# Moving the last two rows' key and value groups, and the output's bias parts, inside an integer attention

## The chip, the core and the metric

The kernel is one launch on one core of a Trainium2 chip. The metric is the device time of that launch in microseconds (us): the median of several runs. Beside it there is one profiled execution, from which every duration below comes. The engines are named as in the profile: PE is TensorE (matmuls and transposes), PEld its loading of weights, DVE is VectorE, ACT is ScalarE, POOL is GpSimd, and SP is SyncE, which issues nearly all DMAs. Each engine runs its own instructions in the order in which they were built, and waits for others by semaphores.

## The reference, cut to what matters

The program is a decoder of two layers, each an attention, a cross attention to media and a feed-forward part, on 8 rows of 512 positions with 256 channels. The change lies in the second layer's attention, which is computed in 8-bit integers, and touches the media attention behind it:

```python
x = x + _L1_attn_ref(_layernorm(x), ...)          # integer attention
x = x + _L1_xattn_ref(_layernorm(x), ctx_1024, ...)   # media attention
x = x + _L1_ffn_ref(_layernorm(x), ...)

# _L1_attn_ref, 16 heads of 16 channels
aw, aws = quant_act(einsum('ntd,nsd->nts', q, k), 8)
probs, ps = int_softmax(aw, aws, 8)
probs, ps = quant_act(probs, 8)
attn, as_ = quant_act(einsum('nts,nsd->ntd', probs, v), 8)   # one scale for all of attn
out = (einsum('tbi,oi->tbo', attn / as_, w_int) + round(b / b_s)) * b_s

# _L1_xattn_ref
k, v = split(media @ Wkv, 2, axis=-1)             # does not depend on x
```

`quant_act` takes the greatest absolute value of the whole tensor as its scale and rounds to integers. So the values of the attention (`attn`) can only be rounded when all of them are there. The keys and values of the media attention depend on `ctx_1024` and weights alone, and can be computed at any time before it.

## The kernel before, in words

**The integer attention** is `stage_quantized_attention`. Its last part runs through these stages, with the times of the profiled execution in us from the start of the span:

- scores (about 2170 to 2205), in eight blocks of 128 x 1024, kept in `aw`;
- softmax in integers (`integer_softmax`, 2205 to 2281), nearly all on DVE with exponents on ACT, ending in a global maximum, `ptop`, and its inverse `pr`;
- probability times value (2281 to 2333): a loop over nine iterations n. `spread(n)` copies the values of block n onto the diagonal of a zeroed tile `vz` (L2614, half on POOL, half on DVE). `turn(n)` rounds the probabilities (L2621, DVE), writes them four times, masked, into `qa_wide` (L2624, four ACT instructions), transposes them (L2632, 16 on PE) and copies the two PSUM tiles into `qa_pT` (L2635, DVE). `weigh(n - 1)` multiplies with the values (L2645, 64 small matmuls), copies the result to `m_` (L2653, ACT) and takes its maximum (L2654, DVE);
- the global maximum of the result and its scales (L2670 to L2678), then the **bias parts**: `bias_parts` (L2374 to L2383, ten DVE operations) rounds the output's bias and splits it into three bf16 parts in one row `brow`, which a matmul adds later; `orow` (L2686) is the row of output scales;
- rounding (about 2336 to 2352): eight blocks, each with one ACT instruction that adds a large constant (L2692), one DVE instruction that takes it off and writes bf16 (`qa_mi`, L2693), and eight transposes (L2696). After each second block eight small copies bring the transposed tiles from PSUM to `mT`; they go through `evac`, which takes ACT (L101) and DVE (L103) in turn;
- output (2351 to 2378): for each row eight matmuls (L2709) with four that add the bias (L2712), a scaling on DVE (`qa_o`, L2714), and the sum into `x` (L2716, on DVE or POOL).

**The media keys and values** of all 8 rows are computed ahead, inside that stage, by `keys_values`, a generator. One of its **groups** is one of four parts of a row's keys or of its values: two matmuls of 128 x 512 in f32 (L2756; each gives two records in the trace), a copy from PSUM to `kv_o`, a tile with three buffers (L2761, ACT), and a store of 256 KB to DRAM (L2762, SP). A row has eight groups, and takes one load of its context (L2733, SP). Row 0 is done during the scores. Rows 1 to 5 are done in the softmax: 40 groups, whose contexts lie in `room`, a large tile that is free then. Rows 6 and 7 are done in the value loop: two groups at the end of each of the first eight iterations, with one buffer, `kv_ctx`, for the context of both rows.

**What sets the order.** The code is recorded in program order, and a tile scheduler orders each engine's instructions; tiles come from pools, and a tile that takes the memory of an earlier one waits for the last use of that one (a store's landing included). Within an engine, the built order is what runs. In the built order of before, L2374 waits only for operations of DVE.

**The media attention**, `stage_media_attention`, starts with loads on SP (L2828, L2830, L2843 for keys and values of a row from DRAM, and L3022 for the router), and with normalizing `x` (L157).

Of the kernel before, what the change touches and what calls it, by code (L numbers as in the profile page):

```python
# [27 lines left out]
F32 = mybir.dt.float32  # L28
# [6 lines left out]
ALU = mybir.AluOpType  # L35
# [4 lines left out]
P = 128  # L40
B, S, C = 8, 512, 256
NST = S // P
# [1235 lines left out]
class FastDecoder(Decoder):  # L1278
# [1108 lines left out]
    def stage_quantized_attention(self, w):  # L2387
        nc, q = self.nc, self.q
        wT, ident, ones, magic = q["wT"], q["ident"], q["ones"], q["magic"]
        tc = self.tc  # L2390
        with tc.tile_pool(reuse_waits="tile", name="qa", bufs=1) as pool:
# [16 lines left out]
            brow = self.alloc(pool, [P, 3 * C], BF16, "qa_brow")  # L2408
            with tc.tile_pool(reuse_waits="tile", name="qa1", bufs=2) as tmp, tc.tile_pool(
                reuse_waits="tile", name="qp1", bufs=1, space=PSUM  # L2410
# [140 lines left out]
            with tc.tile_pool(reuse_waits="tile", name="qa2", bufs=1) as tmp, tc.tile_pool(  # L2551
                reuse_waits="tile", name="qp2", bufs=2, space=PSUM
# [6 lines left out]
                for n in range(8):  # L2559
# [6 lines left out]
                    for m in range(4):  # L2566
                        at = 4 * n + m
# [19 lines left out]
            with tc.tile_pool(reuse_waits="tile", name="qa3", bufs=2) as tmp, tc.tile_pool(  # L2587
                reuse_waits="tile", name="qp3", bufs=4, space=PSUM
            ) as psum:
                ptop = self.integer_softmax(tmp, aw, qs, atop)  # L2590
                room = self.alloc(pool, [P, 8, 2, S], F32, "qa_big")
                for _ in self.keys_values(tmp, psum, range(1, 6), room, "kv", 4):
                    pass

                ps_, _ = self.scaled(pool, ptop, 1.0 / 128.0 / 127.0, "qa_ps")
                pr = one("qa_pr")
                nc.vector.reciprocal(pr, ptop)
                nc.vector.tensor_scalar(pr, pr, 127.0, None, ALU.mult)


            m_ = self.alloc(pool, [P, 8, 4, C], F32, "qa_big")
            mtops = one("qa_mtops", 8)

            vz = h16("vz").rearrange("p (j i m a r d) -> p j i m a r d", j=2, i=NST, m=4, a=4, r=4)
# [1 line left out]
            with tc.tile_pool(reuse_waits="tile", name="qa4", bufs=2) as tmp, tc.tile_pool(  # L2606
                reuse_waits="tile", name="qp4", bufs=1, space=PSUM
            ) as psum:
                held = {}

                def spread(n):
                    for r in range(4):
                        rows_ = slice(32 * r, 32 * r + 32)
                        (nc.gpsimd if r < 2 else nc.vector).tensor_copy(  # L2614
                            vz[rows_, n % 2, :, :, :, r, :].rearrange("p i m a d -> p (i m) a d"),
                            vq[rows_, :, :, n].rearrange("p i m (a d) -> p (i m) a d", d=16),
                        )

                def turn(n):
                    a = aw[:, n]  # L2620
                    nc.vector.tensor_scalar(a, a, pr, MAGIC, ALU.mult, ALU.add)  # L2621
                    wide = self.alloc(tmp, [P, 16, 4, 4, B], BF16, "qa_wide")
                    for k in range(4):
                        nc.scalar.activation(  # L2624
                            wide[:, :, :, k, :].rearrange("p a r s -> p r a s"), a, AF.Identity,
                            bias=q["at_off"][:, k : k + 1], scale=q["at"][:, k : k + 1],
                        )
                    pT = held[n] = self.alloc(tmp, [P, 16, P], BF16, "qa_pT")
                    for half in range(2):
                        ps = self.alloc(psum, [P, 8, P], BF16, "tr", bufs=4)  # L2630
                        for i in range(8):
                            nc.tensor.transpose(  # L2632
                                ps[:, i], wide[:, 8 * half + i].rearrange("p r k s -> p (r k s)"), ident
                            )
                        nc.vector.tensor_copy(pT[:, 8 * half : 8 * half + 8], ps)  # L2635

                def weigh(n):
                    pT = held.pop(n)
                    po = self.alloc(psum, [P, 4, C], F32, "po", bufs=2)
                    for m in range(4):  # L2640
                        for a in range(4):
                            g, e = divmod(a, 2)
                            for st in range(NST):
                                rows_ = slice(32 * st, 32 * st + 32)
                                nc.tensor.matmul(  # L2645
                                    po[rows_, m, g * P : (g + 1) * P].rearrange("p (r e d) -> p e r d", e=2, d=16)[
                                        :, e
                                    ],
                                    pT[:, 4 * m + a, rows_],
                                    vz[:, n % 2, st, m, a].rearrange("p r d -> p (r d)"),  # L2650
                                    start=True, stop=True, skip_group_check=True,
                                )
                    nc.scalar.copy(m_[:, n], po)  # L2653
                    nc.vector.tensor_reduce(  # L2654
                        mtops[:, n : n + 1], m_[:, n], AX.XY, ALU.max, apply_absolute_value=True
                    )

                ahead = self.keys_values(tmp, psum, range(6, B), None, "tr", 4)
                for n in range(9):
                    if n < 8:  # L2660
                        spread(n)
                        turn(n)
                    if n:
                        weigh(n - 1)
                    for _ in range(2):
                        next(ahead, None)


            mtop = one("qa_mpart")
            nc.vector.tensor_reduce(mtop, mtops, AX.X, ALU.max)  # L2670
# [7 lines left out]
            nc.vector.reciprocal(osc_inv, osc)  # L2678
            mT = h16("mT").rearrange("p (c i t m) -> p c i t m", c=2, i=NST, t=B)
            brow = self.alloc(pool, [P, C], BF16, "qa_orow")  # L2680
            self.bias_parts(brow, q["rb"][:, 3 * C :], osc_inv, "qa_b")
            with tc.tile_pool(reuse_waits="tile", name="qa5", bufs=2) as tmp, tc.tile_pool(
                reuse_waits="tile", name="qp5", bufs=1, space=PSUM
            ) as psum:
                orow = self.alloc(tmp, [P, C], F32, "qa_orow_s", bufs=1)
                nc.vector.tensor_scalar(orow, q["wsc"][:, C:], osc, None, ALU.mult)  # L2686
                for n in range(0, 8, 2):
                    ps = [self.alloc(psum, [P, 8, P], BF16, "tr", bufs=4) for c in range(2)]
                    for h in range(2):
                        f = m_[:, n + h]  # L2690
                        mi = self.alloc(tmp, [P, 4, C], BF16, "qa_mi")
                        nc.scalar.activation(f, f, AF.Identity, bias=magic[:, 0:1], scale=mr)  # L2692
                        nc.vector.tensor_scalar(mi, f, -MAGIC, None, ALU.add)  # L2693
                        for c in range(2):
                            for m in range(4):
                                nc.tensor.transpose(  # L2696
                                    ps[c][:, 4 * h + m], mi[:, m, c * P : (c + 1) * P], ident
                                )
                    for c in range(2):
                        for st in range(NST):  # L2700
                            self.evac(
                                mT[:, c, st, :, 16 * n : 16 * n + 32].rearrange("p t (m k) -> p t m k", k=4),
                                ps[c][:, :, 32 * st : 32 * st + 32].rearrange("p m (k t) -> p t m k", t=B),
                            )
                for b in range(B):
                    ps = self.alloc(psum, [P, NST, C], F32, "pj", bufs=2)
                    for st in range(NST):
                        for c in range(2):
                            nc.tensor.matmul(  # L2709
                                ps[:, st], mT[:, c, st, b], wT[:, c, 3 * C :], start=(c == 0), stop=False  # L2710
                            )
                        nc.tensor.matmul(ps[:, st], ones[:, :P], brow, start=False, stop=True)  # L2712
                    o = self.alloc(tmp, [P, NST, C], F32, "qa_o")
                    nc.vector.tensor_tensor(o, ps, orow.unsqueeze(1).broadcast_to([P, NST, C]), ALU.mult)  # L2714
                    x = self.x[:, b * NST : (b + 1) * NST, :]
                    (nc.gpsimd if b in (2, 4, 6) else nc.vector).tensor_tensor(x, x, o, ALU.add)  # L2716
                    if b == 0:
                        self.media_stats = {b: self.twice_normal(tmp, b, self.const)}
        self.integers.close()

    def load_media_attention(self):
        self.w_media = super().load_media_attention()
        return self.w_media

    def keys_values(self, pool, psum, rows, room, tag, bufs, outs=None):

# [792 lines left out]
```

## Time and profile before

| What | us |
|---|---|
| median of 3 runs (3087.45, 3094.61, 3096.63) | 3094.61 |
| the profiled execution's own time | 3094.66 |
| its span, first to last instruction | 3092.7 |
| PE busy | 2842.4 (92%) |
| DVE busy | 2158.3 (70%) |
| ACT busy | 1155.1 (37%) |
| mean granted clock of PE | 0.974 |

The profiled execution is 2.0 us longer than its span. The profile page gives busy times over the whole program; the part that is changed takes some 170 us of it, so the views that matter are those of a stretch of time: busy times by stage, the chain of waits (the work that ended last, followed back to what released it), and the timeline. In a timeline line the first number is the start, the second the busy time, then engine, line and operation, output<-inputs, and in brackets the idle time before it and what ended it. `x8` is the number of instructions joined in a line.

### The profile page before, as it was taken

How to read it: one execution, taken by the hardware profiler on the slowest of the kernel's cores; microseconds unless marked ns; L12 is line 12 of the kernel's file. 1: busy time of each engine (PE TensorE's matmuls, PEld its weight loads, DVE VectorE, ACT ScalarE, POOL GpSimd, SP SyncE). 2: the span in 40 equal slices, each digit the busy share in tenths (PEclk: the TensorE clock that was granted, in tenths of full speed). 3: DMA queues.
4: the chain of work that ended last, by engine and by line, in shares of the span. 5: the costliest groups of instructions: out<-in, count | busy, mean ns of one | idle time of the engine just before them, and what ended most of it. 6: DMA issues, size and time to landing. Idle time of an engine off the chain costs nothing. (4 is left out here: it accounts for less than half of the span.)

```text
span 3092.7 us, 40203 instructions
## 1 busy us (share of the span) xinstructions
PE 2842.4 (92%) x14929; PEld 1507.6 (49%) x14944; DVE 2158.3 (70%) x4962; ACT 1155.1 (37%) x1623; POOL 409.6 (13%) x389
## 2 busy tenths in 40 slices
PE   8999999969999999999999999999786999997998
PEld 5653333225555556555555556555344334434665
DVE  7458999977887894357887898548788766665110
ACT  2237777724334321124344331115263443441111
POOL 1111111100001010000101111112111123231111
PEclk9999999989999999999999999999997999998999
DMA  7011212101001001001000012010332122223231
GB/s 242 1 35 50 71 49 70 36 19 56 15 15 29 15 24 36 0 1 43 22 15 22 22 38 69 14 41 28 125 122 76 52 93 83 90 69 96 98 139 61
DMA packets 130696, 168.74 MB, mean 55 GB/s; under 512 B 51760, under 2 KB 79665, under 8 KB 128442
## 3 DMA queue, kind: packets, MB, share of 16 engines
q1 hardware_dynamic: 126394, 154.48, 16.0%
q0 software_dynamic: 4096, 11.59, 1.0%
q8 instruction: 119, 1.95, 0.3%
q14 instruction: 87, 0.71, 0.1%
HBM read 113.12 MB, written 47.50 MB: 52 GB/s over the span
## 5 line engine op out<-in xcount | busy, mean ns | idle before, releaser
L1885 PE MATMUL pj<-w,la_hT 128*128 128x512 f32 x720 | 342.8, 615 | 32.7 <-DVE x L2062 16.3
L1732 DVE TENSOR_TENSOR x_e<-x_e,x_share 128x1024 f32<-128x1024 f32 x256 | 317.6, 1283 | 16.7 <-ACT x_e L1731 16.5
L1731 ACT ACTIVATE x_e<-sc 128x1024 f32<-128x1024 f32 x256 | 249.4, 1023 | 82.0 <-PE sc L1720 82.0
L1885 PEld LDWEIGHTS pj<-w,la_hT 128*128 128x128 f32 x720 | 131.7, 194 | 189.3 <-issue 118.1
L2007 ACT ACTIVATE la_e<-la_e 128x1024 f32<-128x1024 f32 (+1 forms) x128 | 121.1, 952 | 209.2 <-DVE la_e L2003 209.2
L2890 ACT ACTIVATE ma_e<-sc,ma_bias 128x1024 f32<-128x1024 f32 x128 | 135.8, 1110 | 165.3 <-PE sc L2884 165.3
L2216 ACT ACTIVATE lf_gate<-pj,lf_b 128x512 f32<-128x512 f32 (+1 forms) x82 | 56.3, 687 | 346.6 <-PE pj L2195 337.2
L2897 DVE TENSOR_TENSOR ma_esum<-ma_esum,ma_e 128x1024 f32<-128x1024 f32 x96 | 129.8, 1353 | 71.3 <-ACT ma_e L2890 34.8
L2195 PE MATMUL pj<-lf_hnT,w 128*128 128x512 f32 (+1 forms) x368 | 171.7, 595 | 0.6 <-DVE lf_hid L2221 0.6
L2003 DVE TENSOR_TENSOR la_e<-sc,la_mask 128x1024 f32<-128x1024 f32 (+1 forms) x128 | 137.0, 1081 | 41.1 <-PE sc L1995 41.0
L3262 POOL TENSOR_TENSOR la_oT<-la_o,x_wide 128x512 f32<-128x512 f32 x64 | 88.3, 1387 | 571.0 <-DMA x_wide<-invs 315.4
L1748 PE MATMUL po<-x_e,x_v 128*32 128x512 f32 x1024 | 138.1, 612 | 21.9 <-DVE x_e L1732 15.2
L2195 PE MATMUL sc<-lf_hnT,w 128*128 128x512 f32 x336 | 157.9, 592 | 0.0
L1720 PE MATMUL sc<-x_q,x_k 32*128 32x512 f32 x1024 | 151.3, 640 | 1.7 <-DVE sa_ok L1448 1.4
L2267 PE MATMUL po<-w,lf_hid 128*128 128x256 f32 x640 | 148.8, 379 | 0.0
L2221 DVE SCALAR_TENSOR_TENSOR lf_hid<-sc,lf_b,lf_gate 128x512 f32<-128x512 f32 x70 | 52.4, 748 | 126.9 <-PE sc L2195 126.9
L1995 PE MATMUL sc<-la_qkT 64*128 64x256 f32 (+1 forms) x1024 | 124.2, 373 | 12.3 <-ACT la_qkT L1931 11.3
L1892 ACT ACTIVATE la_sq<-pj 128x512 f32<-128x512 f32 x120 | 71.4, 595 | 170.3 <-PE pj L1885 170.3
L2057 PE MATMUL pj<-w,la_oT 128*128 128x256 f32 x512 | 122.3, 385 | 11.3 <-DVE x L2062 9.4
L2884 PE MATMUL sc<-ma_qT,ma_kT 64*128 64x512 f32 x512 | 129.9, 626 | 0.0
L2267 PEld LDWEIGHTS po<-w,lf_hid 128*128 128x128 f32 x640 | 117.8, 190 | 20.2 <-issue 6.7
L2908 PE MATMUL po<-ma_e,ma_v 128*64 128x512 f32 x512 | 124.2, 606 | 0.0
(493 smaller groups left out, 5296.2 us busy)
## 6 DMA issues: line engine op xcount, KB each, us to landing
x_wide<-invs SPq DMA_DIRECT2D x184, 128.0 KB
w<-in_f_w_dram SPq DMA_DIRECT2D x16, 1024.0 KB
kv<-kv_o SPq DMA_DIRECT2D x56, 256.0 KB
slots<-x_empty SPq DMA_DIRECT2D x8, 1028.0 KB
x_mask<-in_x_maskT_dram SPq DMA_DIRECT2D x8, 1024.0 KB
ma_kT<-kv SPq DMA_DIRECT2D x8, 1024.0 KB
ma_v<-kv SPq DMA_DIRECT2D x8, 1024.0 KB
ex_rows<-slots SPq DMA_DIRECT2D x7, 1028.0 KB
```

What stands on the lines that cost most here:

```text
L1720: nc.tensor.matmul(pair[r // 2][:, r % 2, :], d["k"][rows, g, kt * P : (kt + 1) * P], d["q"][rows, e, g, :], start=True, stop=True,)
L1731: nc.scalar.activation(ex, d["e"][rest][p], AF.Exp)
L1732: nc.vector.tensor_tensor(ex, ex, d["share"][:, kt, :].unsqueeze(1).broadcast_to([P, 2, 512]), ALU.mult)
L1748: nc.tensor.matmul(d["po"][32 * r : 32 * r + 32, :], d["v"][:, kt, 8 * g + 2 * r + e, :], ex[r // 2][:, r % 2, :], start=(kt == 0), stop=( ...
L1885: nc.tensor.matmul(ps, d["hT"][:, k, i * P : (i + 1) * P], wqkv[:, k, j * S : (j + 1) * S], start=(k == 0), stop=(k == 1),)
L1995: nc.tensor.matmul(both[half][:, r, jj * 256 : jj * 256 + to - j * P], d["qkT"][rows, 4 + c, j * P : (j + 1) * P], d["qkT"][rows, c, j * P ...
L2003: nc.vector.tensor_tensor(ex[:, :, :n_cols], ps[:, :, :n_cols], mask[:, :n_cols].unsqueeze(1).broadcast_to([P, 2, n_cols]), ALU.add,)
L2195: nc.tensor.matmul(ps[:m, :], w1[:, k, at : at + m], held[b]["hnT"][:, k, :], start=(k == 0), stop=(k == 1))
L2267: nc.tensor.matmul(ps[:, :C], held[b]["hid"][:, f, i * P : (i + 1) * P], w2[:, f, :], start=(f == 0), stop=False,)
L2884: nc.tensor.matmul(both[m // 2][:, r, :], d["k"][rows, c, kt * P : (kt + 1) * P], d["q"][rows, c, :], start=True, stop=True,)
L2890: nc.scalar.activation(ex, ps, AF.Exp, bias=bias[:, b * NST + kt : b * NST + kt + 1], scale=0.125)
L2897: nc.vector.tensor_tensor(d["sum", c], d["sum", c], ex, ALU.add)
```

## The change

Three things are changed in `stage_quantized_attention`:

- The sixteen groups of rows 6 and 7 are no longer made by the generator, but one at a time by a new function, `project`, from a list. Five are recorded at the end of the softmax, behind the 40 of rows 1 to 5. In the value loop one is recorded in each iteration but those with n = 3 and n = 7 (seven), and two behind the loop. The last two are recorded in the first two rows of the output. Row 6's context goes into `room`, row 7's into a tile of its own.
- The bias parts and the row of output scales are recorded behind the evacuations of the second pair of rounded blocks (n == 2), instead of ahead of all rounding.
- `m_`, which holds the result of the value loop, is a view of `room` instead of a new tile of the same tag.

In the built order of after, the five copies of the groups in the softmax stand ahead of the first L2624 on ACT; the bias parts are spread over DVE's order between the second L2693 and the seventh, among evacuations; and the tile that L2374 writes takes memory that `kv_o` of the value loop had.

```diff
@@ softmax
+                ctx6 = self.context(room[:, 5], 6)
+                groups = [(ctx6, 6, j, g) for j in range(2) for g in range(NST)]
+
+                def project(tmp, psum, tag, count=1):
+                    for group in groups[:count]:
+                        self.keys_values_group(tmp, psum, *group, tag, 4)
+                    del groups[:count]
+
+                project(tmp, psum, "kv", 5)
@@ ahead of the value loop
-            m_ = self.alloc(pool, [P, 8, 4, C], F32, "qa_big")
+            m_ = room.rearrange("p n a s -> p n (a s)").rearrange("p n (m c) -> p n m c", c=C)
+            stay = ExitStack()
+            late = stay.enter_context(tc.tile_pool(reuse_waits="tile", name="qx", bufs=1))
+            ctx7 = self.context(self.alloc(late, [P, 2, S], F32, "qa_ctx"), 7)
+            groups += [(ctx7, 7, j, g) for j in range(2) for g in range(NST)]
@@ value loop
-                ahead = self.keys_values(tmp, psum, range(6, B), None, "tr", 4)
                 for n in range(9):
                     if n < 8:
                         spread(n)
                         turn(n)
                     if n:
                         weigh(n - 1)
-                    for _ in range(2):
-                        next(ahead, None)
-
+                    if n % 4 != 3:
+                        project(tmp, psum, "tr")
+                project(tmp, psum, "tr", 2)
@@ rounding
-            self.bias_parts(brow, q["rb"][:, 3 * C :], osc_inv, "qa_b")
...
-                nc.vector.tensor_scalar(orow, q["wsc"][:, C:], osc, None, ALU.mult)
...
+                    if n == 2:
+                        self.bias_parts(brow, q["rb"][:, 3 * C :], osc_inv, "qa_b")
+                        nc.vector.tensor_scalar(orow, q["wsc"][:, C:], osc, None, ALU.mult)
@@ output, for each row behind its matmuls
+                    project(tmp, psum, "tr")
...
+            stay.close()
@@ new methods
+    def context(self, out, b):
+        self.nc.sync.dma_start(
+            out, self.t["ctxT"].rearrange("(k p) n -> p k n", p=P)[:, :, b * S : (b + 1) * S]
+        )
+        return out
+
+    def keys_values_group(self, pool, psum, ctxT, b, j, g, tag, bufs):
+        nc, wkv = self.nc, self.w_media[1]
+        ps = self.alloc(psum, [P, 1, S], F32, tag, bufs=bufs)
+        at = slice(g * P, (g + 1) * P)
+        for k in range(2):
+            w, x = wkv[:, k, j * S : (j + 1) * S], ctxT[:, k, :]
+            w, x = (w[:, at], x) if j == 0 else (x[:, at], w)
+            nc.tensor.matmul(ps[:, 0], w, x, start=(k == 0), stop=(k == 1))
+        o = self.alloc(pool, [P, 1, S], F32, "kv_o", bufs=3)
+        nc.scalar.copy(o, ps)
+        nc.sync.dma_start(self.kv[b, j][:, g * S : (g + 1) * S], o.rearrange("p a n -> p (a n)"))
```

## The prediction

> **What bounds the kernel now.** I read the busy shares first, then the forty slices, the chain of waits over the integer attention, the busy times by stage, and last the timeline of each engine where two stages meet. Over the whole run TensorE is the bound:
>
> ```profile
> PE 2842.4 (92%) x14929; PEld 1507.6 (49%) x14944; DVE 2158.3 (70%) x4962; ACT 1155.1 (37%) x1623; POOL 409.6 (13%) x389
> ```
>
> But the change touches only some 170 us of integer attention, and there each stage has its own limit. Busy times by stage (columns as in the first line): softmax, probability times value, rounding and transposing.
>
> ```profile
> core 0: us, PE busy (x) PEld busy (x) DVE busy (x) ACT busy (x) POOL busy (x), PEclk, DMA share, GB/s
> 2205.00:2277.00 72.00, 71.07 (x160) 31.12 (x160) 61.91 (x108) 35.79 (x52) 0.31 (x1) 0.97 0.44 165
> 2284.50:2336.00 51.50, 45.01 (x704) 25.79 (x704) 34.25 (x41) 36.35 (x52) 13.24 (x13) 0.93 0.29 96
> 2336.00:2352.00 16.00, 8.61 (x69) 6.80 (x70) 14.03 (x37) 13.79 (x24) 0.00 (x0) 0.50 0.45 190
> ```
>
> In the softmax TensorE has only the groups of rows 1 to 5 and is full with them (71.07 of 72), yet they are beside VectorE's chain. In the value loop TensorE is the bound, in the rounding VectorE and ScalarE in turns. The chain of waits says the same in order of time (start, length, what; lines left out between):
>
> ```profile
> 2297.56 3.63 PE tr L2756 x8
> 2302.70 3.63 PE tr L2756 x8
> ...
> 2306.86 4.47 DMA kv_ctx<-in_ctxT_dram
> ...
> 2311.47 5.37 PE tr L2756 x8
> ...
> 2331.99 0.67 PE po L2645 x64
> 2332.69 1.02 ACT qa_big L2653
> ...
> 2336.09 6.91 ACT qa_big L2692 x6
> ...
> 2354.18 2.36 DVE qa_o L2714 x2
> ```
>
> The reader is to see three things: two groups per iteration (3.63 us) are the largest piece of each iteration of 5.14 us (2302.70 − 2297.56); at row 7 the single buffer of the context stops the chain for 4.47 us, and the next groups run slowly (5.37 for 3.63); and the stage leaves for the output product at 2354.18. The media attention's first normalization is at 2378.65. Single instructions, from the timeline (start, busy, engine, line, in brackets the idle time before and its releaser):
>
> ```profile
> 2227.06 0.59 ACT L2761 COPY kv_o<-kv 128x512 f32<-128x512 f32 x1 [1.16 <-DMA kv<-kv_o]
> 2276.62 0.58 ACT L2761 COPY kv_o<-kv 128x512 f32<-128x512 f32 x1 [1.13 <-PE kv L2756]
> 2281.52 7.86 ACT L2624 ACTIVATE qa_wide<-qa_aw,qw_at_off,qw_at 128x512 bf16<-128x512 f32 x11 [4.31 <-DVE qa_aw L2621]
> 2296.53 1.29 DVE L2635 COPY qa_pT<-tr 128x1024 bf16<-128x1024 bf16 x2 [0.27 <-PE tr L2632]
> 2297.85 2.31 DVE L2614 COPY qa_h<-qa_h 32x1024 bf16<-32x1024 bf16 x2
> 2300.19 1.22 DVE L2654 TENSOR_REDUCE qa_mtops<-qa_big 128x1 f32<-128x1024 f32 x1
> 2336.35 0.35 DVE L2374 TENSOR_SCALAR qa_b_v<-qw_rb,qa_osc_r 128x256 f32<-128x256 f32 x1
> 2340.29 1.29 DVE L2693 TENSOR_SCALAR qa_mi<-qa_big 128x1024 bf16<-128x1024 f32 x2
> ```
>
> **What the Trainium skill says.** "TensorE: Matmul & The Clock Gate", section "Architectural detail: the array is 16× 32×32, not 1× 128×128", says that ScalarE and VectorE are strict first-in first-out queues. The trace agrees: the copy at 2227.06 stands 1.16 us for its buffer's store, and ScalarE runs nothing past it. So the built order tells who waits. The same page, "What's actually happening", says that after an idle window of about 3.4 us the clock falls to half. The trace agrees: behind the DMA wait at 2306.86 the next eight matmul records take 5.37 us for 3.63, single ones up to 1.06 us for 0.59. [...]Here the store freed the buffer at 2227.04 whose copy ended at 2224.94 (first of three, starting at 2224.36): 2.1 us. I use 2.1.
>
> **The change part by part.** Sixteen groups (rows 6 and 7) move; none goes away. A group is 1.72 us on TensorE (four records, 0.43 apart), 0.59 on ScalarE, one store on SP.
>
> *A, softmax: five groups more.* TensorE ends there at 2276.54; five more end it at 2276.54 + 5 × 1.72 = 2285.1. VectorE is done with the softmax at 2281.5 as before, but in the built order the five copies stand ahead of the first spread of the probabilities (L2624): last copy 2285.15 to 2285.75, first spread 2285.8 instead of 2281.52. **+4.3.** It would be nothing if the scheduler had put them behind. The context of row 6 is loaded on SP behind three stores, about 2213, sixty us ahead of its use.
>
> *B, value loop.* Of the sixteen groups seven stay: iterations 0, 1, 2, 4, 5, 6, 8 have one, 3 and 7 none. Row 7's context has its own buffer and is issued as the loop starts (about 2286), used from iteration 4 (2307 or later): a load of 4.47 us is hidden, so the 4.47 us and the slow records behind it go. TensorE then needs 0.89 transposes + 0.69 products + 1.72 + 0.17 gaps = 3.5 per iteration. What is late next is VectorE: 1.29 (L2635) + 2.31 (L2614) + 1.22 (L2654) = 4.82; ScalarE 4 × 0.74 + 1.02 + 0.59 = 4.6. So the period is 4.82. Counted from the first spread: the transposes of iteration 0 start at +3.0 (as 2281.52 to 2284.50), those of iteration 1 at +7.1 (two sets of spreads 5.9, a copy 0.6, a handover 0.6), the first eight are read at +8.2, L2635 of iteration 2 starts at 8.2 + 4.82 + 0.1 = +13.1, of iteration 7 at 13.1 + 5 × 4.82 = +37.2, and the last products (L2645 of n = 7) at 37.2 + 1.29 + 0.1 = +38.6, as no groups stand ahead of them any more. Before: 2331.99 − 2281.52 = 50.4 (L2645 shows at 2331.92 in the timeline). **−11.8.** The last products start at W = 2285.8 + 38.6 = 2324.4.
>
> *C, rounding.* Three groups stand behind the last products; TensorE is free there. Their copies do not come free: in ScalarE's order they lie between the first roundings (L2692, 1.15 each). First rounding at W + 4.2 as before, two copies more between the first three: +1.2. The bias parts (11 operations L2374 to L2383 and the output row, 2336.35 to 2340.3: 4.0 us) leave the place ahead of the first L2693, but VectorE mostly waited for ScalarE's roundings there, and now stand behind the second L2693. And they bring a wait: their tile takes the memory of a copy's buffer, so L2374 waits for the last store. That copy ends at W + 7.7, its store lands 2.1 later, W + 9.8; VectorE is ready at W + 7.9: 1.9 us of standing. Queued behind on VectorE: the third L2693 and the evacuations of the transposes, which alternate with ScalarE's, so both engines wait. Bounds for the standing: nothing, if the store lands as the copy ends plus 0.2, to 4.3, with a landing like the 4.47 us load; I take 1.9. One L2692 more stands before ScalarE's first evacuation: at W + 13.4 instead of W + 11.0 (2342.89). From there both engines are near full (14.03 and 13.79 of 16), and the bias work that had been under ScalarE's lead lies between the evacuations: the last one ends about W + 25.0 to 25.8 instead of W + 20.9 (2352.8). One matmul of a group stands ahead of the output product, 0.9. Output product at W + 27.1 instead of 2354.18 − 2331.92 = 22.3. **+4.8**, bounds +1.5 (no standing, half of the bias parts covered) and +7.2.
>
> *D, output.* The last two groups go under VectorE's chain from 2354 to 2378 (22.42 of 24 busy; TensorE 12.91): 3.4 us on TensorE, 1.2 on ScalarE (0.34 busy). Nothing; if TensorE went cold there it would cost up to 3. On SP the last stores now stand ahead of the loads of the media stage (bias and router rows, keys and values of row 0), which so move from 2333 to about 2356. Three such loads of 1 MB had landed within 10 us; the keys are used at 2391, the values at 2398: some 20 us of margin. Nothing.
>
> The sum: 4.3 − 11.8 + 4.8 = **−2.7 us**, against the profiled execution's 3094.66 (span 3092.7 and 2.0 around it): 3092.0. The median of the runs, 3094.61, is the same within 0.05, so the forecast is **3092**. What follows the stage keeps its order and shifts rigidly.
>
> **The rivals.**
> 1. *As summed*, 3092; with the bounds of C (+1.5 to +7.2) and 2 us for the ramp of B, 3087 to 3098. For it: the built order of both queues. Chance 0.60.
> 2. *The rounding is not lengthened*: the store lands under cover and the evacuations take the bias parts into their gaps (VectorE 2 and ScalarE 2.2 us free of 16). Then 4.3 − 11.8 = −7.5 → 3087; with the copies in A behind the first spread, down to 3083. Against: both engines almost full. Chance 0.20.
> 3. *Slower: the clock falls in the thinned loop.* TensorE would be busy only 3.5 of 4.82 us. For it: the clock is 0.50 in 2341 to 2351, where only transposes run; sixteen of them took 1.89 at 2284.50, behind 8 us of idleness, and 0.89 later. At half clock an iteration with a group is 1.89 + 1.2 + 3.4 = 6.5, without one 3.2: from the second on, 6 × 6.5 + 2 × 3.2 = 45.6 instead of 38.6, +7.0 → 3099. It decides once the cold iteration passes VectorE's 4.82. Against: such an iteration makes TensorE full again, and the clock stayed at 1.00 in 2356 to 2366 at 2.23 to 2.78 busy of 5. Chance 0.12.
> 4. *No effect on the end*: the media stage starts by something else, 3094.7. Against: the chain runs unbroken into it. Chance 0.08.
>
> **How the numbers follow.** 0.3%, 9.3 us, is about what a measurement of this kernel can tell from no change (the runs span 9.2). Below 3085.3: half of case 2 and the tail of case 1, 0.13. Above 3103.9: a third of case 3 and a little of case 1, 0.06. The rest 0.81. Range: case 1's own, widened down by half of case 2 and up to case 3: 3084 to 3100.
>
> **What would show it.** Last ScalarE copy of the softmax at 2285.7 and L2624 right behind; iterations 4.8 apart with VectorE full and no DMA wait; last products at 2324 to 2325; L2374 standing for a store for about 2 us; ScalarE's first evacuation 13.4 behind the last products; output product near 2351.5, first normalization near 2376. It is wrong if the first spread keeps 2281.5 (then −7), if the clock in the loop is under 0.9 (then slower), or if L2374 waits over 4.5 us.

## The result, and the profile after

| | before | after |
|---|---|---|
| median of 22 runs each, us | 3093.03 | 3084.62 |
| lowest and highest, us | 3082.83 to 3101.04 | 3078.49 to 3098.72 |
| profiled execution, us | 3094.66 | 3091.44 |
| its span, us | 3092.7 | 3089.4 |

The ratio of after to before is 0.9977, with a 95% interval of 0.9966 to 0.9988: about 7.1 us less (3.7 to 10.5). The forecast was 2.7 us less, 3092, with a range of 3084 to 3100. The median of after lies inside that range, 0.6 us above its lower end.

Runs of one kernel differ by 20 us, and the traces show where. The code up to the softmax's maximum is nearly the same in all fourteen kernels of this case, and yet it ends between 2273.1 and 2287.7 in their traces; from the media attention's first normalization to the end the fourteen take 714 to 719 us. Inside the changed stage distances repeat far better, though not equally well. The last of the four steps below takes 24.06 to 24.14 us in all eight kernels that have at most two groups there. The third takes 19.19, 19.43 and 19.30 us in the three kernels that are alike in it before the change, but 23.72, 23.71 and 24.46 us in three that are alike in it after. So the steps are measured inside the trace, one profiled execution for each kernel, and a difference under half a microsecond is not taken for an effect. The five marks are: the softmax's maximum (`is_ptop` on DVE), the first spread (`qa_wide` on ACT), the result's maximum (`qa_mpart` on DVE), the first output product (`qa_o`), the media attention's first normalization (`ma_xn`, L157).

| from, to | before, us | after, us | difference | forecast |
|---|---|---|---|---|
| A softmax's maximum, first spread | 1.74 | 5.89 | +4.15 | +4.3 |
| B first spread, result's maximum | 53.47 | 36.64 | −16.83 | −11.8 |
| C result's maximum, output product | 19.19 | 23.72 | +4.53 | +4.8 |
| D output product, first normalization | 24.14 | 24.07 | −0.07 | 0 |
| sum | 98.54 | 90.32 | −8.22 | −2.7 |

The forecast divides B from C at the last products instead of the result's maximum; so divided, B went from 50.4 to 33.2 us and C from 22.3 to 27.1. The stage explains the result: −8.2 us against −7.1 with its interval. The profiled pair alone would say −3.2, because the unchanged code behind the stage took 718.4 us in this execution (3089.4 − 2371.05) and 714.4 in that of before.

Busy times by stage, after: the value loop in the window shown of before, three of its iterations, and the output (columns as in the first line).

```profile
core 0: us, PE busy (x) PEld busy (x) DVE busy (x) ACT busy (x) POOL busy (x), PEclk, DMA share, GB/s
2284.50:2336.00 51.50, 38.01 (x715) 23.13 (x714) 34.34 (x60) 46.44 (x65) 13.09 (x13) 0.87 0.20 70
2304.49:2317.12 12.63, 10.86 (x253) 6.48 (x253) 11.46 (x19) 12.63 (x19) 7.99 (x8) 1.00 0.13 45
2347.00:2371.00 24.00, 13.44 (x90) 9.55 (x89) 23.41 (x49) 1.17 (x2) 8.37 (x5) 0.85 0.54 198
```

The second line is the one that decides: from one set of transposes (2304.49) to the third after it (2317.12) there are 12.63 us, 4.21 an iteration instead of 5.14, and ScalarE is busy for all of it. VectorE is busy for 11.46 us of it. The bound of the loop has gone from TensorE to ScalarE, with VectorE close behind. The chain of waits of this execution ends in the output's last transfers and does not reach back to these stages, so the single instructions are read from the timeline of after:

```profile
2286.13 0.59 ACT L2757 COPY kv_o<-kv 128x512 f32<-128x512 f32 x1 [1.13 <-PE kv L2755]
2286.62 7.86 ACT L2638 ACTIVATE qa_wide<-qa_aw,qw_at_off,qw_at 128x512 bf16<-128x512 f32 x11
...
2295.04 0.59 ACT L2757 COPY kv_o<-tr 128x512 f32<-128x512 f32 x1 [0.57 <-PE tr L2755]
...
2297.03 2.20 POOL L2628 COPY qa_h<-qa_h 32x1024 bf16<-32x1024 bf16 x2 [15.70 <-PE po L2659]
2297.27 2.25 DVE L2628 COPY qa_h<-qa_h 32x1024 bf16<-32x1024 bf16 x2
...
2300.45 2.13 POOL L2628 COPY qa_h<-qa_h 32x1024 bf16<-32x1024 bf16 x2 [1.22 <-PE po L2659]
2300.69 1.28 DVE L2649 COPY qa_pT<-tr 128x1024 bf16<-128x1024 bf16 x2
...
2309.41 0.87 DVE L2628 COPY qa_h<-qa_h 32x1024 bf16<-32x1024 bf16 x2
...
2310.56 2.13 POOL L2628 COPY qa_h<-qa_h 32x1024 bf16<-32x1024 bf16 x2 [1.76 <-PE po L2659]
...
2312.76 0.87 DVE L2628 COPY qa_h<-qa_h 32x1024 bf16<-32x1024 bf16 x2
...
2330.07 0.35 DVE L2374 TENSOR_SCALAR qa_b_v<-qw_rb,qa_osc_r 128x256 f32<-128x256 f32 x1 [2.13 <-ACT qa_big L2703]
...
2333.25 0.63 ACT L101 COPY qa_h<-tr 128x256 bf16<-128x256 bf16 x2
...
2342.36 2.02 PE L2755 MATMUL tr<-w,qa_ctx 128*128 128x512 f32 x2
...
2346.98 1.22 DVE L2729 TENSOR_TENSOR qa_o<-pj,qa_orow_s 128x1024 f32<-128x1024 f32 x1 [2.68 <-PE pj L2726]
```

The reader is to see five things:

- The first spread stands right behind the last copy, as forecast.
- From there to the last spread, which ends at 2317.07, ScalarE stands idle only once, for 0.57 us.
- The two VectorE copies that took 2.31 us before (L2614, now L2628) take 2.25 beside GpSimd's, and 0.87 with GpSimd not copying (its copies at 2310.56 end at 2312.69). VectorE's copy out of PSUM (L2649) is not stretched beside GpSimd's: 1.28 us at 2300.69.
- L2374 stands 2.13 us. The line names ScalarE's rounding, which had ended at 2327.21; in the built order the tile also takes memory of the groups' copies, and so waits for their stores. The trace doesn't name the store.
- A group's first matmul stands ahead of the first output product and takes 2.02 us, for 1.12 at 2346.74: the granted clock is 0.50 from 2338 to 2347.

### The profile page after: what moved, and what is told of

The parts are those of the page before. It is cut to its first block, busy times and chain, and to the rows that moved or that the text cites. A ratio compares the mean times of both kernels' runs of the same rounds, so it can differ in the third digit from the quotient of the medians.

```text
span 3089.4 us, 40204 instructions
## 1 busy us (share of the span) xinstructions
PE 2852.6 (92%) x14929; PEld 1511.8 (49%) x14944; DVE 2150.4 (70%) x4962; ACT 1155.5 (37%) x1623; POOL 415.3 (13%) x389
## 5 line engine op out<-in xcount | busy, mean ns | idle before, releaser
L1731 ACT ACTIVATE x_e<-sc 128x1024 f32<-128x1024 f32 x256 | 249.5, 1024 | 81.1 <-PE sc L1720 80.6
L2014 PE MATMUL po<-la_e,la_v 128*64 128x256 f32 (+1 forms) x1024 | 118.3, 370 | 7.4 <-ACT la_o L2031 4.9
```

The source lines that it names most:

```text
L1731: nc.scalar.activation(ex, d["e"][rest][p], AF.Exp)
```

## The experiments

Each is timed against the kernel before, but the readings rest on the marks, of one profiled execution each.

**Context alone.** The kernel before, with only the single buffer of the context taken away:

```diff
-            m_ = self.alloc(pool, [P, 8, 4, C], F32, "qa_big")
+            m_ = room.rearrange("p n a s -> p n (a s)").rearrange("p n (m c) -> p n m c", c=C)
...
-                ahead = self.keys_values(tmp, psum, range(6, B), None, "tr", 4)
+                ahead = self.keys_values(tmp, psum, range(6, B), room[:, 6:], "tr", 4)
```

> The kernel before with one part of the change: the contexts of rows 6 and 7 lie in the large tile and are both loaded early; two groups per iteration as before. Theory (the value loop's gain is in two parts, the context wait and the thinning): the 4.47 us wait and the slow records behind it (1.7 us) go, iterations stay at 5.14 us as TensorE is full; first spread of probabilities to last products 50.4 less 6.2 = 44.2 us, output product 6 us earlier, time 6 us less (ratio 0.998). VectorE's copies L2614 stay at 2.3 us per iteration, as GpSimd's run at the same time. Rival (the context wait only stood in for another wait): 50 us, ratio 1.000.

Measured: ratio 0.9990 (0.9976 to 1.0004). First spread to the result's maximum 48.51 us instead of 53.47, so the context wait is worth 5.0 of the 16.8 us of B (6.2 were expected), and the transposes of the eight iterations are 5.14 us apart from the second on (2286.38, 2291.52, 2296.66, ...). VectorE's copies stay at 2.31 to 2.38 us. Four of these iterations:

```profile
2291.52:2312.09 20.57, 20.57 (x353) 11.97 (x352) 19.27 (x21) 19.46 (x29) 8.61 (x8) 1.00 0.29 104
```

TensorE is full (20.57 of 20.57). The other 11.9 us of B are left for the thinning of the groups and what it sets free; they are the difference and were not measured by themselves.

**Who slows VectorE's copies.** All four value copies of an iteration on VectorE, in the changed kernel and in the kernel before:

```diff
-                        (nc.gpsimd if r < 2 else nc.vector).tensor_copy(
+                        nc.vector.tensor_copy(
```

> The changed kernel with all four value copies of an iteration on VectorE instead of two on GpSimd. Theory (a VectorE copy takes about 0.43 us alone and 1.15 us only while GpSimd copies at the same time): four copies 1.75 us per iteration, VectorE 4.3, the loop stays at ScalarE's pace of about 4.2 us, first spread to last products 33 to 34 us, ratio as the changed kernel, 0.9977. Rival (a copy takes 1.15 us by itself): four copies 4.6 us, VectorE 7.1 us per iteration, the loop 17 us longer, ratio 1.003.

> The kernel before with all four value copies of an iteration on VectorE. Theory (the 2.3 us for two copies in the kernel before are contention with GpSimd): four take 1.75 us, iterations stay at 5.14 us since TensorE is the bound, time unchanged, 3094. Rival (1.15 us each by themselves): 4.6 us for four, VectorE 7.1 us per iteration, 12 us more.

Measured in the changed kernel: ratio 0.9975 (0.9959 to 0.9992). Four copies take 1.75 to 1.77 us, less than two beside GpSimd's, and the iterations stay 4.21 us apart. First spread to the last products was expected at 33 to 34 us (33.2 in the changed kernel) and took 35.6; to the mark it is 39.11, 2.5 more than in the changed kernel. That is the loop's end: the last transposed block stands on VectorE behind four copies and a maximum, and the last products wait for it. Timeline of this run:

```profile
2325.22 1.77 DVE L2628 COPY qa_h<-qa_h 32x1024 bf16<-32x1024 bf16 x4
...
2327.02 1.22 DVE L2668 TENSOR_REDUCE qa_mtops<-qa_big 128x1 f32<-128x1024 f32 x1
...
2328.15 1.28 DVE L2649 COPY qa_pT<-tr 128x1024 bf16<-128x1024 bf16 x2
2328.89 0.42 PE L2659 MATMUL po<-qa_h,qa_pT 128*32 128x64 bf16 x32 [3.02 <-DVE qa_pT L2649]
```

The sum of this run's marks, 97.19 us, can't be set beside the others'. Its A is 9.56 us: in its ScalarE order two copies of groups instead of four stand ahead of the softmax's first rounding (L2827), so the maximum comes earlier against TensorE's groups, and the first spread still waits for the fifth copy.

Measured in the kernel before (a single run, 3099.98 us, from which no time is concluded): the same 1.76 us for four, at the old pace of 5.14. B is 56.58 us there, 3.1 more, where the groups behind the two loads of the context take 6.16 and 6.41 us for 4.73 and 5.37.

```profile
2296.84 1.29 DVE L2635 COPY qa_pT<-tr 128x1024 bf16<-128x1024 bf16 x2 [0.28 <-PE tr L2632]
2298.04 1.76 DVE L2614 COPY qa_h<-qa_h 32x1024 bf16<-32x1024 bf16 x4
2300.49 1.22 DVE L2654 TENSOR_REDUCE qa_mtops<-qa_big 128x1 f32<-128x1024 f32 x1 [0.68 <-ACT qa_big L2653]
2301.98 1.29 DVE L2635 COPY qa_pT<-tr 128x1024 bf16<-128x1024 bf16 x2 [0.28 <-PE tr L2632]
```

So a copy takes 0.44 us by itself, and 1.1 us, the length of one of GpSimd's, when GpSimd copies at the same time. The Trainium skill has a cause for this in "SBUF — State Buffer", section "SBUF: two separate sides": VectorE and GpSimd share a pair of ports that is an exclusive lock, held for a whole instruction, while the other "fully blocks". It says so of VectorE's operations in a two-port mode or with two inputs in SBUF, not of all; the trace agrees, as the copy out of PSUM at 2300.69 keeps its 1.28 us. In the kernel before both engines' copies are released by the same products and collide in every iteration; GpSimd's beside VectorE's at 2297.85 is

```profile
2297.66 2.21 POOL L2614 COPY qa_h<-qa_h 32x1024 bf16<-32x1024 bf16 x2 [2.94 <-PE po L2645]
```

In the changed kernel VectorE comes to its copies later, and its six pairs take 2.25, 1.32, 1.02 and three times 0.87 us.

**The bias parts in their two places.** Back ahead of the rounding in the changed kernel, and moved alone in the kernel before:

```diff
             brow = self.alloc(pool, [P, C], BF16, "qa_orow")
+            self.bias_parts(brow, q["rb"][:, 3 * C :], osc_inv, "qa_b")
...
-                    if n == 2:
-                        self.bias_parts(brow, q["rb"][:, 3 * C :], osc_inv, "qa_b")
-                        nc.vector.tensor_scalar(orow, q["wsc"][:, C:], osc, None, ALU.mult)
```

(The first run's diff; the row of scales goes back too. The second run's is the change's own part of it.)

> The changed kernel with the bias parts back ahead of the rounding. Theory (the bias parts' new place, with its wait for a store, is most of what the rounding got longer): last products to output product falls from 27.1 to 24.4 us (22.3 of before, two copies 1.2, one matmul of a group 0.9), time 2.7 us under the changed kernel, ratio to before about 0.9968. Rival (the copies of groups between the roundings are the cost, the bias parts are covered in either place): 27 us, ratio as the changed kernel, 0.9977.

> The kernel before with only the bias parts moved behind the first rounded blocks. Theory (VectorE's work on the bias comes out from under ScalarE's lead and lies between evacuations; no store is waited for, since the last one has landed): last products to output product from 22.3 to 24 or 25.5 us, time 2 to 3 us more, ratio 1.0008. Rival (the move alone costs nothing, or gains since the first rounded block no longer stands behind 4 us of bias work): 22.3 us or less, ratio 1.000 or below.

Measured: back in the old place ratio 0.9978 (0.9965 to 0.9992), result's maximum to output product 23.86 us instead of 23.72: nothing. My theory falls. Moved alone: ratio 1.000 (0.9989 to 1.0011), too small for the runs, but by the marks 17.47 us instead of 19.19: a gain of 1.7, where I had expected a loss. Timeline of the kernel with the bias moved alone:

```profile
2343.51 4.64 ACT L2690 ACTIVATE qa_big<-qa_big,qw_magic,qa_mr 128x1024 f32<-128x1024 f32 x4 [2.39 <-DVE qa_mr L2674]
...
2343.90 0.35 DVE L2374 TENSOR_SCALAR qa_b_v<-qw_rb,qa_osc_r 128x256 f32<-128x256 f32 x1
...
2348.06 0.61 ACT L101 COPY qa_h<-tr 128x256 bf16<-128x256 bf16 x2
```

Four roundings (4.64 us) stand ahead of ScalarE's first evacuation instead of six (6.91 in the chain of before), as the order was built; L2374 waits for nothing that shows. The first evacuation comes 5.65 us behind the result's maximum instead of 7.90. And in the changed kernel with the bias in the old place:

```profile
2326.95 1.24 ACT L2705 ACTIVATE qa_big<-qa_big,qw_magic,qa_mr 128x1024 f32<-128x1024 f32 x1
...
2328.10 0.57 ACT L2756 COPY kv_o<-tr 128x512 f32<-128x512 f32 x1
...
2328.56 6.90 ACT L2705 ACTIVATE qa_big<-qa_big,qw_magic,qa_mr 128x1024 f32<-128x1024 f32 x6
...
2335.36 0.62 ACT L101 COPY qa_h<-tr 128x256 bf16<-128x256 bf16 x2
```

Two copies of groups and all eight roundings stand ahead of the first evacuation, which comes 11.12 us behind the result's maximum. So the place of the bias parts is not what C costs; that leaves the copies and the order that they bring about, which the next run takes away.

**The groups behind the loop.** The changed kernel without them; they go to the output, which has four:

```diff
-                project(tmp, psum, "tr", 2)
```

> The changed kernel with the two groups behind the value loop moved to the output (four there instead of two). Theory (the copies between the roundings, the roundings ordered ahead of the first evacuation because of them, and the wait for their store are what the rounding got longer): from the result's maximum to the first output product 23.7 falls to 17.5 us, the value of the kernel before with the bias moved alone, or to 19 with TensorE at half clock; time 5 us under the changed kernel, ratio 0.996. Rival (the slow clock of TensorE and the group ahead of the output product are the cost): 22 us or more, ratio 0.9975.

Measured: ratio 0.9963 (0.9943 to 0.9983). First evacuation 5.64 us behind the result's maximum (9.99 in the changed kernel, 5.65 with the bias moved alone): the copies and the wait for their store are gone. The output product follows 20.08 us behind the maximum: 3.6 less, not the 6 I expected, though more than the rival allowed. Of the 2.6 us over 17.47, 2.2 are VectorE's wait for TensorE right ahead of the product: 2.68 us here and 0.50 with the bias moved alone. Timeline of this run:

```profile
2344.37 2.02 PE L2754 MATMUL tr<-w,qa_ctx 128*128 128x512 f32 x2
2348.99 1.23 DVE L2728 TENSOR_TENSOR qa_o<-pj,qa_orow_s 128x1024 f32<-128x1024 f32 x1 [2.68 <-PE pj L2725]
```

The same with the bias moved alone:

```profile
2359.88 2.36 DVE L2715 TENSOR_TENSOR qa_o<-pj,qa_orow_s 128x1024 f32<-128x1024 f32 x2 [0.50 <-PE pj L2713]
```

Here a group's first matmul, at half clock, stands ahead of the first row's, and these run slowly too. The output itself takes 26.17 us instead of 24.07, so that the stage, 88.69 us, is 1.6 shorter than with the change.

**The groups in the softmax.** None there, seven in the output. With this edit three groups of row 6 are computed from a context that the result has already overwritten, so part of the media keys and values is changed, and one group waits for the copy that overwrites its context.

```diff
-                project(tmp, psum, "kv", 5)
```

> The changed kernel with none of its five groups in the softmax; the groups move up one place each, and seven instead of two are left for the output. Theory (the five copies hold ScalarE's first spread up, and the output has room): last softmax result to first spread falls from 5.9 to 1.7 us, the output stays at 24 us with TensorE at about 21 of 24 us, time 4 us under the changed kernel, ratio to before 0.9963. Rival (TensorE becomes the bound of the output): first output product to the media attention's first normalization grows from 24 to 28 us or more, and the ratio stays at 0.9977.

Measured: ratio 0.9977 (0.9966 to 0.9988). Term A falls to 1.68 us, as forecast: the five copies are all of it. But the loop takes 38.78 us (2.1 more) and the output 26.77 (2.7 more), 90.37 in all: nothing is won. In the loop a group at half clock stands ahead of the last transposes:

```profile
2305.37 3.60 PE L2754 MATMUL tr<-w,qa_big 128*128 128x512 f32 x4 [0.76 <-ACT qa_big L2666]
```

It waits for ScalarE's copy of the result into its context, which is this edit's own doing, so how much of the 2.1 us another place for that context would save isn't known. The granted clock is 0.52 here, behind 3.3 us in which TensorE was busy for 0.71. The rival was right on the sum; of its mechanism, an output longer by 4 us or more, 2.7 came.

**Copies on VectorE.** The seven copies of groups in the loop on VectorE instead of ScalarE:

```diff
-                        project(tmp, psum, "tr")
+                        project(tmp, psum, "tr", copy=nc.vector.tensor_copy)
...
-        nc.scalar.copy(o, ps)
+        copy(o, ps)
```

> The changed kernel with the seven copies of groups in the value loop on VectorE instead of ScalarE. Theory (ScalarE's 4.2 us per iteration paces the loop, since VectorE's value copies take 0.87 us when GpSimd is late): ScalarE 3.7, VectorE 4.0, first spread to the result's maximum falls from 36.6 to about 34.5 us, ratio 0.997. Rival (VectorE's 4.8 us as forecast paces the loop): 7 times 0.6 more, 40.8 us, ratio 0.999.

Measured: ratio 0.9975 (0.9964 to 0.9986). 39.32 us, between the two: iterations of about 4.0 us in the second half, since VectorE now has 1.28 + 0.87 + 1.22 + 0.68, but 9.3 us instead of 6.1 from the last transposes to the result's maximum, because the last block stands behind VectorE's queue again, and a group's copy stands ahead of the maximum itself. That the iterations got shorter agrees with ScalarE as the bound at 4.21. The sum does not tell the bounds apart; they are nearly equal.

**Together.** Three groups in the softmax, seven in the loop, six in the output, the bias in its new place:

```diff
-                project(tmp, psum, "kv", 5)
+                project(tmp, psum, "kv", 3)
...
-                project(tmp, psum, "tr", 2)
```

> The changed kernel with three groups in the softmax, seven in the value loop, none behind it, and six in the output. Theory (costs of the copies in the softmax and in the rounding are avoided and the output has room): softmax result to first spread 2.5 us, result's maximum to output product 17.5 to 19 us, output 24 to 25 us; softmax result to first normalization 82 to 84 us for 98.5 before and 90.3 with the change; ratio 0.995. Rival (TensorE is the bound of the output, or the loads of the media stage come too late behind the stores): output 28 us or a wait in front of the media attention's first scores, ratio 0.997 or more.

Measured: ratio 0.9961 (0.9947 to 0.9974). A 2.44, B 35.81, C 19.58, D 26.77: 84.60 us, a little over the forecast. The output:

```profile
2334.30:2361.00 26.70, 19.98 (x106) 12.13 (x104) 25.50 (x48) 3.52 (x6) 8.01 (x5) 0.87 0.44 163
```

VectorE is busy for 25.50 us, 2.1 more than in the changed kernel's output (23.41 us). Most of that is GpSimd again. In this run's timeline two operations of 128 x 4 that take 0.16 us elsewhere last as long as GpSimd's sum that starts with them (2.35 and 2.34 us); one of them:

```profile
2349.57 0.16 DVE L3040 TENSOR_SCALAR ma_var<-ma_var 128x4 f32<-128x4 f32 x1
2349.77 2.34 DVE L1473 TENSOR_SCALAR ma_rstd<-ma_var 128x4 int32<-128x4 int32 x1
2352.14 0.16 DVE L1475 SCALAR_TENSOR_TENSOR ma_t<-ma_rstd 128x4 f32<-128x4 f32 x1
```

```profile
2349.73 2.35 POOL L2730 TENSOR_TENSOR x<-x,qa_o 128x1024 f32<-128x1024 f32 x1 [5.56 <-DVE ma_var L3040]
```

Together with a sum stretched from 1.23 to 1.83 us that is 5.0 us of waiting. The changed kernel's output has three such waits too, of 1.1 to 1.2 us each, 3.4 together. So they make 1.5 of the 2.7 us that its output is longer; the rest isn't shown.

Three further variants: the groups from the output's second row on; the combination with the bias parts in the old place; and, with the groups from the second row, one of the four spreads on VectorE. The first one's edit:

```diff
-                    project(tmp, psum, "tr")
+                    if b:
+                        project(tmp, psum, "tr")
```

> Three groups in the softmax, seven in the value loop, none behind it, and six in the output, but from its second row on instead of the first. Theory (a group's first matmul, at TensorE's half clock 2 us, stands ahead of the first output product): result's maximum to output product falls from 19.6 to about 18 us, the output stays at 26.8; softmax result to first normalization 83 us for 98.5 before, 90.3 with the change and 84.6 with the first row; ratio to before 0.9955. Rival (the group takes nothing that isn't waited for anyhow, or the output gets longer by the same): 84.6 us, ratio 0.9961.

> The combination with three groups in the softmax, seven in the loop and six in the output, with the bias parts back ahead of the rounding. Theory (the bias parts' new place gains where no store is waited for): result's maximum to output product 19.6 plus 1.7 = 21.3 us. Rival (the place of the bias parts costs nothing either way): 19.6 us.

> As the run with groups from the second output row, and one of the four spreads of the probabilities of each iteration on VectorE instead of ScalarE. Theory (ScalarE's 4.2 us paces the loop, VectorE has 3.4 us): ScalarE 3.5, VectorE 3.9 to 4.1, first spread to the result's maximum from 35.8 to 33 or 34 us, ratio 0.995. Rival (VectorE's order holds the transposes up, or its copies meet GpSimd's again and take 2.3 us): 37 us or more, ratio 0.996 or more.

Measured, groups from the second row: ratio 0.9955 (0.9939 to 0.9971), C 19.13 (0.45 less, not 1.6), D 26.30, the stage 83.69: the shortest here, 6.6 us shorter than with the change, though the runs do not tell it from the combination. But the theory was not tested: in the built order of this kernel too a group's first matmul stands ahead of the first row's.

```profile
2338.32 2.02 PE L2755 MATMUL tr<-qa_ctx,w 128*128 128x512 f32 x2
```

And in the kernel with a spread on VectorE, which has its groups from the second row as well, C is 19.57 us, as in the combination. Bias in the old place: C 21.67 instead of 19.58, so its new place is worth 2.1 us in C where no store stands in its way (a single run, 3086.71 us). In the whole stage 0.7 is left of it (85.33 us instead of 84.60), as the output takes 25.40 us there instead of 26.77. One spread on VectorE, where its edit is

```diff
+                        if k == 3:
+                            nc.vector.tensor_scalar(out, a, at, off, ALU.mult, ALU.add)
+                            continue
```

took 38.04 us for B instead of 35.79, ratio 0.9972 (0.9962 to 0.9983): the rival's case. VectorE's copies meet GpSimd's again:

```profile
2306.72 2.06 DVE L2628 COPY qa_h<-qa_h 32x1024 bf16<-32x1024 bf16 x2
2308.81 0.55 DVE L2641 TENSOR_SCALAR qa_wide<-qa_aw,qw_at,qw_at_off 128x512 bf16<-128x512 f32 x1
...
2316.33 0.87 DVE L2628 COPY qa_h<-qa_h 32x1024 bf16<-32x1024 bf16 x2
```

## Why the prediction was right or wrong

The direction held, and the time lies in the range, near its lower end. The gain was under-forecast, 2.7 us for 7.1 (8.2 by the marks), and nearly all of that is in one part, B.

- **A was right**, +4.15 for +4.3, and by its mechanism: without the five groups it is 1.68 us.
- **B had the right parts and its period mis-sized.** The context wait and the thinning are both there (5.0 and 11.9 us). The step that failed is "VectorE: 1.29 (L2635) + 2.31 (L2614) + 1.22 (L2654) = 4.82 ... So the period is 4.82". The 2.31 was read off a profile in which GpSimd copies at that moment: a wait for GpSimd inside a busy time. In the changed kernel it falls from 2.25 to 0.87 by the fourth iteration that has it. From L2649 of iteration 2 (2300.69) to that of iteration 7 (2319.13) there are 18.4 us, where 4.82 would give 24.1. On VectorE the five pairs of copies between them took 4.95 us instead of 11.55, 6.6 less, and 1.0 of that went into waits for ScalarE. The ramp up to iteration 2 took 1.0 us more than forecast.
- **But the 2.31 alone does not give the number.** Without it the forecast's next bound, ScalarE's 4.6, would have set the period, and by the same steps the last products would stand at 37.3 us instead of 38.6; they stood at 33.2. ScalarE's term was mis-sized too. It adds 0.74 for each of four spreads, 1.02 and 0.59, but where they follow each other their starts lie 0.71, 0.89 and 0.47 apart, as each overlaps the next: 4.2 an iteration. One of the iterations has no group, and ScalarE had worked ahead while TensorE was slow at the start (eleven spreads in a row at 2286.62). So the transposes from the third set on follow each other by 3.43, 2.39 and then three times 4.21 us. The same distances appear with all four value copies on VectorE. That ScalarE's queue sets them is read from its being full; no run shortened that queue without loading VectorE. The bounds I gave had no entry for either term, since I took every duration in the loop as fixed.
- **C was right as a number for a wrong reason.** The forecast +4.8 came from the two copies (1.2), the standing (1.9) and the bias work lying among the evacuations. The standing was there, 2.13 us, and the first evacuation came 13.4 us behind the last products, as forecast. But the bias parts cost nothing in their new place: alone it gains 1.7 us, without groups behind the loop 2.1 in C, and in the changed kernel nothing is left of that gain (23.72 and 23.86 us), which the 2.13 us of standing would explain. That the number came out at +4.8 is luck to this extent. The cost belongs to the groups behind the loop, by the copies and the extra rounding ahead of the first evacuation (together first evacuation 9.99 us behind the result's maximum for 7.90), and to the slow end of the stage. There the one matmul of a group ahead of the output product was priced at 0.9 us and held TensorE for 1.8 at half clock. How the 2.6 us of that end split between this group and the slow matmuls of the first row stays open, as every run with groups in the output has one ahead of the first product.
- **D was right** for two groups, −0.07. (Its 22.42 and 12.91 of 24 are those of 2352 to 2376; from 2354 to 2378 VectorE has 23.28 and TensorE 10.91.) It is no free room: four cost 2.1 us, six 2.7, or 1.3 with the bias in the old place.
- **The rivals.** The rival of the **cold loop** did not come: in the three iterations shown the clock is 1.00. Single groups at half clock (3.6 to 3.7 us) do occur, at the loop's start, which brings the clock from the first transposes to the last products down to 0.90, and, in the run without groups in the softmax, near its end. The rival of an **unlengthened rounding** gave 7.5 us less, closest to the 7.1 measured, for the wrong reason: the rounding was lengthened, and the loop gained more. That **the end was set elsewhere** is excluded by the marks, and by the ratios of 0.9961 and 0.9955, 12 and 14 us, for stages 13.9 and 14.9 us shorter.

## What to carry to other kernels

A busy time is not a price: VectorE's held its wait for GpSimd, and that wait goes when an edit shifts the two apart, so price an operation from a row in which its neighbour is idle. Price a full queue by the distance from start to start, not by the sum of busy times. Work that is "hidden" behind a loop still stands in an in-order queue; look at what the built order puts ahead of the first instruction that others wait for. When whole runs scatter by more than the effect, measure between marks inside the stage, and see first how well each distance repeats in kernels that are alike there.

## What the runs showed of the hardware

- VectorE's busy time holds its wait for GpSimd: two 32 x 1024 bf16 copies take 0.87 us alone and 2.1 to 2.38 us beside GpSimd's two of 2.2, four alone 1.75, and an operation of 128 x 4 takes 2.34 us beside a sum of 2.35 on GpSimd. A copy out of PSUM keeps 1.28 us beside GpSimd's copies.
- On ScalarE an instruction's busy time overlaps the next one's. In the loop of after a spread shows 0.81 us, but the next starts 0.71 behind its start; a copy of the result shows 1.01 for 0.89, a group's copy 0.59 for 0.47.
- The clock can halve without a long gap: 0.52 behind 3.3 us in which TensorE was busy for 0.71, in gaps of at most 1.8; at 10.86 busy of 12.63 it stayed at 1.00.
- The output repeats within 0.1 us between executions (24.06 to 24.14), the TensorE-bound code ahead of the stage does not (2273.1 to 2287.7 at the same mark).
- L2374, whose tile takes memory that groups' copies had, began 2.4 us behind the end of the last of these copies (2327.69 to 2330.07). Without groups behind the loop it did not stand at all. A store's landing fits both, but no line names it.
